# A two-layer image block: copies moved to one queue, and a new order of the second layer's steps

## The chip, the cores and the metric

The kernel runs on one core of a Trainium2 chip. The metric is the device time of one execution in microseconds (us). A core has five engines that run side by side, each in its own order of instructions: TensorE (PE, with its weight loads PEld), VectorE (DVE), ScalarE (ACT), GpSimd (POOL) and SyncE (SP), which here only issues transfers. Semaphores hold an instruction until what it needs is there.

## The reference, cut to what matters

32 images of 96 channels, 56 x 56. Two residual layers, each behind a group normalisation over three channels at a time:

```
# layer 0, on v = groupnorm(x): 4-bit weights and activations
h = act_q(bn(conv1x1(v, w1, 96 -> 576)))        # expansion
h = act_q(bn(depthwise3x3(h, w2)))
x = x + v + bn(conv1x1(h, w3, 576 -> 96))       # projection

# layer 1, on v = groupnorm(x): three parts of 32 channels; the gates come from means of v
a = conv3x3(v[:32],   conv0_w  * gate)          # spatial
F = frft2d(v[32:64], alpha)                     # fractional Fourier transform, alpha from an MLP
b = |frft2d(conv1x1([Re F, Im F], conv05_w * gate), -alpha)| / (56 * 56)
c = irfft2(conv1x1(rfft2(v[64:]), conv1_w * gate))
x = x + v + conv3x3([a, b, c], conv2_w)         # the finals
```

## The kernel before, in words

**Layer 0 of an image** works by phases: the 56 x 56 image is four images of 28 x 28 (even or odd row, even or odd column; `k` = 0 to 3). `norm` takes statistics of the input (L333). `split` writes the normalised phases into two tiles, `vh` and `vl`, whose sum is the value (L353 to L362); each has one buffer, so the next image's split can't start before this image's last expansion. `expand(b, k)` multiplies a phase with a block of 128 hidden channels (`b` = 0 to 4; block 4 has 64 real channels and 64 of zeros; L372), and `quant_act` takes the result out of PSUM: ScalarE scales and clips below into `qt` (L313), VectorE clips above into an FP8 tile (L315), here one of three `q1s` tiles. Then small copies (L385) rearrange it: 32 channels of one phase go to partitions 32k to 32k + 31 of a `qp` tile (three of these, used in turn by block), so that a depthwise step finds four phases of 32 channels on its 128 partitions. Copies with even group number are issued by SyncE, the others by GpSimd, 72 an image in all. `depthwise(b, j)` (L398) makes 32 of 576 channels, and again `quant_act` follows. `project` (L414) accumulates all 18 groups in PSUM, in two halves of the image, and VectorE adds the result to x (L426); `stats` takes layer 1's statistics of x (L430).

**Layer 1 of an image**: `means`, `gates` and `norm` (the head) give the statistics, the gates, and the normalised parts `xm`, `xf` and `xq`. `weights` makes the gated weights, `angles` the fractional matrices from alpha; its last result goes to two rows of `xf` by four small transfers (L603). `mix_t` and `hilbert` are the Fourier part, `spatial` the 3 x 3 part. The fractional part is `mix_f` (L653: a matmul for each of four pieces of each half image, a copy into a `zs` tile of two buffers, a transfer to `z` in DRAM), then transfers from `z` to `zh` (L663, one image row on each partition) and to `az` (L671), `rows_f` (L678), `columns_f` (L702) and `magnitude` (the roots, L720), which writes a third of `cat`. `final(j)` (L746, `j` = 0 to 6) is the last convolution of eight image rows, from `cat`, and VectorE adds it to x (L754). `store` writes x out (L757).

**Order.** Each step is an entry (cost, function), and `interleave(a, b)` merges two lists in proportion to summed cost. Layer 0 of image i runs beside layer 1 of image i - 1. For each image there are three stages: `conv` (18 depthwise steps and the expansions still missing, with the next image's `norm` and `split` put in) merged with layer 1's steps but the last four finals; `last` (project, stats) merged with two finals; then the head of layer 1 and the next image's first seven expansions (`LEAD`) with the last two finals and the store. The written order is not quite the executed one: the framework's scheduler places the instructions of each engine by its own estimate of times, and keeps what depends on what.

PSUM: `ps0` has two pairs of banks, which expansion, depthwise and projection share; `ps1` has four banks for the rest.

Of the kernel before, what the change touches and what calls it, by code (L numbers as in the profile page):

```python
# [63 lines left out]
LEAD = 7  # L64
L = 57
# [38 lines left out]
def block_kernel(ctx: ExitStack, tc: tile.TileContext, out: bass.AP, a: dict):  # L104
# [8 lines left out]
    p3 = ctx.enter_context(tc.tile_pool(name="p3", bufs=3))  # L113
    dp = ctx.enter_context(tc.tile_pool(name="dp", bufs=2, space=bass.MemoryType.DRAM))
# [28 lines left out]
    def prepare():  # L143
# [32 lines left out]
        w1 = cp.tile([C, NB * 128], F32R, tag="w1r", name="w1r")  # L176
        nc.vector.memset(w1f[:, HID:], 0.0)
        nc.vector.tensor_copy(w1, w1f)
# [74 lines left out]
    for k in range(3):  # L253
        t = cp.tile([128, PH, PW], FP8, tag=f"q1s{k}", name=f"q1s{k}")
        nc.gpsimd.memset(t, 0.0)
        q1s.append(t)
# [68 lines left out]
    def layer0(i):  # L325
# [42 lines left out]
        def expand(b, k):  # L368
            ps = pair(f"pe{i}_{b}_{k}")
            for n, v in enumerate((s["vh"], s["vl"])):  # L370
                for h in range(2):
                    nc.tensor.matmul(  # L372
                        ps[:, h, :HN],
                        w1[:, 128 * b : 128 * (b + 1)],
                        v[:, k, HN * h : HN * (h + 1)],
                        start=(n == 0),
                        stop=(n == 1),
                    )
            src = q1s[turn["q1s"] % 3]
# [53 lines left out]
        ex = [(0.75, lambda b=b, k=k: expand(b, k)) for b in range(NB) for k in range(4)]  # L433
# [16 lines left out]
    def layer1(i):  # L450
# [193 lines left out]
        def mix_f(j):  # L644

            if j == 0:
                s["z"] = dp.tile([128, 2, HH], F32, tag="z", name=f"z{i}")
            at = slice(HN * j, HN * (j + 1))
            for h in range(2):
                t = p2.tile([128, HN], F32, tag="zs", name=f"zs{i}_{j}_{h}")  # L650
                rows = slice(LOW * h, LOW * h + G + 2)
                ps = bank(ps1, f"pm{i}_{j}_{h}")
                nc.tensor.matmul(ps[:, :HN], g1[rows], s["xf"][rows, at], start=True, stop=True)  # L653
# [319 lines left out]
```

## Time and profile before

| | |
|---|---|
| median of 14 runs | 4777.9 us (4737.69 to 4801.65) |
| the profiled execution's own time | 4778.75 us |
| its span, first to last instruction | 4777.0 us |
| TensorE's mean granted clock | 0.942 |
| busy share: PE, DVE, ACT, POOL | 91%, 50%, 45%, 18% |
| finals (L746) on TensorE | 4032 instructions, 1650.9 us |
| depthwise (L398) on TensorE | 4608 instructions, 941.6 us |
| copies to qp (L385): SyncE, GpSimd | 1152 and 1152, of 26.2 KB each |
| longest chain of waits, share of the span | PE 62%, DMA 13%, DVE 10%, ACT 10% |

How to read it: an engine's line gives its busy time and what ended the idle time ahead of its instructions ("PE pi L678 <- DMA zh<-z" is TensorE waiting at line 678 for a transfer from z into zh). `pe`, `pd`, `pp`, `pm`, `pi`, `pz`, `ps` and `pc` are the PSUM results of expansion, depthwise, projection, fractional mix, rows, columns, spatial part and finals; `qte` and `qtd` are ScalarE's results of expansion and depthwise. The granted clock is the share of TensorE's full clock that its throttle let through; a matmul takes correspondingly longer. An instruction of TensorE shown as x18 for one final is nine taps with two passes each.

### The profile page before, as it was taken

What the parts mean: (1) busy time and instruction counts of PE and PEld (TensorE: products, weight loads), DVE (VectorE), ACT (ScalarE), POOL (GpSimd) and SP (SyncE); (2) the same over time, 40 slices, a digit from 0 to 9 for tenths busy, and PEclk for the clock granted to TensorE, in tenths of its full rate; (3) what the DMA queues carried; (4) which work ended last, traced back from release to release, by engine and by line L of the source; (5) the groups of instructions that cost most, each with busy time, mean ns of one, the idle gap of its engine ahead of it and who ended that gap; (6) DMA issues with size and microseconds to landing.
All of it is one profiled execution on the core that took longest, in us unless ns stands there. A gap on an engine that the chain in (4) does not pass through costs nothing.

```text
span 4777.0 us, 60944 instructions
## 1 busy us (share of the span) xinstructions
PE 4327.7 (91%) x21632; PEld 2505.7 (52%) x21632; DVE 2387.4 (50%) x5385; ACT 2168.1 (45%) x2824; POOL 859.5 (18%) x1361
## 2 busy tenths in 40 slices
PE   3899999999999999998999999999989989999987
PEld 2554555555555545555555555555555455555544
DVE  5545454545545544555455454555455444554532
ACT  3544445544445534455344454444454444553431
POOL 3221111221102211112211022211122111122100
PEclk9899999999999989999999999999999999999987
DMA  2221122221222211222212222112223112222112
GB/s 72 44 64 43 30 61 61 64 60 35 40 59 65 64 44 28 60 61 64 55 40 40 59 64 64 52 39 43 61 64 64 47 29 57 61 64 59 33 28 48
DMA packets 378818, 249.65 MB, mean 52 GB/s; under 512 B 283233, under 2 KB 371668, under 8 KB 372372
## 3 DMA queue, kind: packets, MB, share of 16 engines
q1 hardware_dynamic: 339072, 211.72, 20.2%
q0 software_dynamic: 36864, 31.04, 2.8%
q8 instruction: 174, 2.85, 0.3%
q10 hardware_dynamic: 2580, 2.99, 0.2%
q14 instruction: 128, 1.05, 0.1%
HBM read 92.90 MB, written 89.92 MB: 38 GB/s over the span
## 4 chain that ended last, share of the span: by engine, by line
PE 62%; DMA 13%; DVE 10%; ACT 10%; issue 3%; SPq 1%; POOL 1%; DVEq 0%; ACTq 0%; POOLq 0%
PE pc L746 33%; PE pd L398 11%; PE pp L414 5%; DMA z<-zs 5%; DMA zh<-z 4%; PE pe L372 4%; PE pi L678 3%; ACT cat L720 2%; ACT qte L313 2%; DMA xf<-vv 2%; ACT qtd L313 2%; DVE bn L333 2%; DVE x L426 2%; PE px L616 1%; DVE q1s L315 1%
## 5 line engine op out<-in xcount | busy, mean ns | idle before, releaser
L746 PE MATMUL pc<-cat,wc 96*96 96x448 f32 x4032 | 1650.9, 565 | 56.0 <-ACT cat L720 56.0
L385 POOL DMA_DIRECT2D qp<-q1s x1152 | 620.3, 542 | 3646.5 <-issue 1600.1
L746 PEld LDWEIGHTS pc<-cat,wc 96*96 96x96 f32 x4032 | 673.8, 170 | 911.7 <-issue 829.8
L313 ACT ACTIVATE qtd<-pd,o,s 128x784 int16<-128x784 f32 x576 | 577.0, 1002 | 941.0 <-PE pd L398 892.4
L398 PE MATMUL pd<-qp,dw 128*128 128x392 fp8e4 x4608 | 941.6, 349 | 41.5 <-ACT qtd L313 41.5
L313 ACT ACTIVATE qte<-pe,o,s 128x784 int16<-128x784 f32 x640 | 640.0, 1000 | 626.7 <-PE pe L372 608.7
L398 PEld LDWEIGHTS <-dw 128*128 128x128 fp8e4 x4608 | 446.7, 101 | 501.5 <-issue 257.5
L372 PE MATMUL pe<-vh,w1r 96*128 96x392 f32 x1280 | 432.8, 421 | 120.1 <-ACT qte L313 66.1
L315 DVE TENSOR_SCALAR q1s<-qte 128x784 fp8e4<-128x784 int16 x640 | 357.7, 559 | 175.0 <-ACT qte L313 125.2
L754 DVE SCALAR_TENSOR_TENSOR x<-pc,bc,x 96x448 f32<-96x448 f32 x224 | 152.3, 680 | 585.0 <-PE pc L746 582.5
L315 DVE TENSOR_SCALAR q<-qtd 128x784 bf16<-128x784 int16 x576 | 207.3, 360 | 398.8 <-ACT qtd L313 398.7
L372 PE MATMUL pe<-vl,w1r 96*128 96x392 f32 x1280 | 353.1, 358 | 0.0
L372 PEld LDWEIGHTS pe<-vh,w1r 96*128 96x128 f32 x1280 | 226.8, 200 | 238.3 <-issue 103.0
L414 PE MATMUL pp<-q,w3q 32*96 32x392 bf16 x4608 | 254.4, 327 | 2.2 <-DVE x L426 2.2
L372 PEld LDWEIGHTS pe<-vl,w1r 96*128 96x128 f32 x1280 | 247.4, 199 | 0.5
L653 PE MATMUL pm<-xf,g 34*128 34x392 f32 x512 | 187.8, 577 | 49.8 <-DMA xf<-vv 44.2
L426 DVE SCALAR_TENSOR_TENSOR x<-pp,s,x 96x392 f32<-96x392 f32 x256 | 142.3, 616 | 174.3 <-PE pp L414 174.3
L414 PEld LDWEIGHTS <-w3q 32*96 32x96 bf16 x4608 | 180.1, 117 | 85.8 <-issue 32.5
L678 PE MATMUL pi<-cs,zh 120*120 120x112 f32 x1024 | 157.7, 324 | 64.6 <-DMA zh<-z 62.1
L726 PE MATMUL ps<-xq,g 128*128 128x392 f32 x512 | 202.4, 538 | 0.0
L678 PEld LDWEIGHTS pi<-cs,zh 120*120 120x120 f32 x1024 | 152.6, 237 | 75.5 <-DVE q1s L315 29.5
L361 ACT CAST vh<-v 96x392 fp32r<-96x392 f32 x256 | 126.1, 515 | 131.8 <-DVE v L353 131.0
(150 smaller groups left out, 4052.3 us busy)
## 6 DMA issues: line engine op xcount, KB each, us to landing
z<-zs SPq DMA_DIRECT2D x256, 196.0 KB
x<-in_x_dram SPq DMA_DIRECT2D x32, 1176.0 KB
out_dram<-x SPq DMA_DIRECT2D x32, 1176.0 KB
qp<-q1s SPq DMA_DIRECT2D x1152, 26.2 KB
qp<-q1s POOLq DMA_DIRECT2D x1152, 26.2 KB, 1.9
zh<-z SPq DMA_DIRECT2D x64, 392.0 KB
az<-z SPq DMA_DIRECT2D x256, 98.0 KB
xf<-vv SPq DMA_DIRECT2D x128, 6.1 KB
```

The source lines that it names most:

```text
L313: nc.scalar.activation(t.rearrange("p (h n) -> p h n", h=2), ps[:, :, :HN], AF.Relu, bias=offset, scale=scale)
L315: nc.vector.tensor_scalar(dst, src, 15.0, None, ALU.min, saturate=False if dst.dtype == FP8 else None)
L372: nc.tensor.matmul(ps[:, h, :HN], w1[:, 128 * b : 128 * (b + 1)], v[:, k, HN * h : HN * (h + 1)], start=(n == 0), stop=(n == 1),)
L385: (nc.gpsimd if g % 2 else nc.sync).dma_start(out=qps[(NB * i + b) % 3][G * k : G * (k + 1), g, at : at + PH * PW], in_=src[g * G : (g + 1 ...
L398: nc.tensor.matmul(ps[:, h, :HN], dw[:, g, t, :], view(qps[(NB * i + b) % 3][:, j, :], at, [[PW, PH // 2], [1, PH]]), start=(t == 0), stop ...
L414: nc.tensor.matmul(s["pp"][k // 2][:C, k % 2, :HN], w3[rows, g, :], s["q2"][rows, g, HN * h : HN * (h + 1)], start=(g == 0), stop=(g == NG ...
L426: nc.vector.scalar_tensor_tensor(part, src, A3, part, ALU.mult, ALU.add)
L653: nc.tensor.matmul(ps[:, :HN], g1[rows], s["xf"][rows, at], start=True, stop=True)
L678: nc.tensor.matmul(ps[: LOW + W, 2 * W * k : 2 * W * (k + 1)], zh[:, c : c + 2, :].rearrange("p c w -> p (c w)")[:, : LOW + W], cs, start= ...
L726: nc.tensor.matmul(ps[:, :HN], s["g0"][:, 128 * k : 128 * (k + 1)], view(xq, PH // 2 * h * (W + 2) + k, [[W + 2, PH // 2], [2, PH]]), star ...
L746: nc.tensor.matmul(ps[:C, :CN], wc[:, C * t : C * (t + 1)], cat[:, CR * j + dy : CR * j + dy + CR, dx : dx + W], start=(t == 0), stop=(t = ...
L754: nc.vector.scalar_tensor_tensor(part, ps[:C, :CN], bc, part, ALU.add, ALU.add)
```

## The change

All copies to `qp` are issued by SyncE, and there are five `q1s` tiles (`NQ`) instead of three. The scratch space that the program reserves for descriptors of GpSimd's transfers is 1 KB instead of 16. Block 4 is packed: its weights lie between two blocks of zeros, so that four accumulated matmuls put phase k into the lower 64 rows of a PSUM pair and phase k + 1 into the upper 64; one `quant_act` takes both out, and there are 18 expansions an image instead of 20. (The per-channel vectors of block 4 are laid out twice to match, in a helper on the host's side that is left out below.)

In layer 1, `angles` comes ahead of `weights`; `mix_f` is eight steps, ordered by halves of the image, with its own pool of four `zs` buffers (shared with the columns' squares), and each half of `zh` is fetched as soon as its four pieces are written; both spatial steps come ahead of `hilbert`; the roots are taken in two halves, each behind two of the four column steps. Four finals (`HOLD`) are kept for the head instead of two, so one final instead of three lies in `conv`. The next image's statistics go in behind 16 entries of `conv` instead of 8, its split behind 22 instead of 26.

```diff
--- before.py
+++ after.py
@@ -62,6 +62,8 @@
 HH = HW // 2
 LOW = 64
 LEAD = 7
+NQ = 5
+HOLD = 4
 L = 57
 MAGIC = 1.5 * 2.0**23
 TWO_PI = 6.283185
@@ -111,6 +113,7 @@
     p1 = ctx.enter_context(tc.tile_pool(name="p1", bufs=1))
     p2 = ctx.enter_context(tc.tile_pool(name="p2", bufs=2))
     p3 = ctx.enter_context(tc.tile_pool(name="p3", bufs=3))
+    p4 = ctx.enter_context(tc.tile_pool(name="p4", bufs=4))
     dp = ctx.enter_context(tc.tile_pool(name="dp", bufs=2, space=bass.MemoryType.DRAM))
     ps0 = ctx.enter_context(tc.tile_pool(name="ps0", bufs=2, space=PSUM))
     ps1 = ctx.enter_context(tc.tile_pool(name="ps1", bufs=4, space=PSUM))
@@ -173,9 +176,11 @@
 
         w1f = load_tmp("w1")
         quantise(w1f, C, HID, "1")
-        w1 = cp.tile([C, NB * 128], F32R, tag="w1r", name="w1r")
-        nc.vector.memset(w1f[:, HID:], 0.0)
-        nc.vector.tensor_copy(w1, w1f)
+        w1 = cp.tile([C, NB * 128 + 64], F32R, tag="w1r", name="w1r")
+
+        nc.vector.memset(w1[:, HID - 64 :].bitcast(F32), 0.0)
+        nc.vector.tensor_copy(w1[:, : HID - 64], w1f[:, : HID - 64])
+        nc.vector.tensor_copy(w1[:, HID : HID + 64], w1f[:, HID - 64 : HID])
         w2 = load_tmp("w2")
         quantise(w2, 128, NG0 * 16, "2")
         mask = load_tmp("mask")
@@ -250,7 +255,7 @@
 
 
     q1s, qps = [], []
-    for k in range(3):
+    for k in range(NQ):
         t = cp.tile([128, PH, PW], FP8, tag=f"q1s{k}", name=f"q1s{k}")
         nc.gpsimd.memset(t, 0.0)
         q1s.append(t)
@@ -366,26 +371,31 @@
             nc.vector.tensor_scalar(xt, xt, s["one"], s["off"], ALU.mult, ALU.add)
 
         def expand(b, k):
+
             ps = pair(f"pe{i}_{b}_{k}")
-            for n, v in enumerate((s["vh"], s["vl"])):
+            m = blk(b)
+            n = 128 // m
+            for e in range(2 * n):
                 for h in range(2):
+                    at = 128 * b + m * (n - 1) * (1 - e // 2)
                     nc.tensor.matmul(
                         ps[:, h, :HN],
-                        w1[:, 128 * b : 128 * (b + 1)],
-                        v[:, k, HN * h : HN * (h + 1)],
-                        start=(n == 0),
-                        stop=(n == 1),
+                        w1[:, at : at + 128],
+                        s["vl" if e % 2 else "vh"][:, k + e // 2, HN * h : HN * (h + 1)],
+                        start=(e == 0),
+                        stop=(e == 2 * n - 1),
                     )
-            src = q1s[turn["q1s"] % 3]
+            src = q1s[turn["q1s"] % NQ]
             turn["q1s"] += 1
             quant_act(ps, A1[:, b : b + 1], B1[:, b : b + 1], src[:, :, :PH], f"e{i}_{b}_{k}")
 
-            n, at = blk(b) // G, PW * (k // 2) + k % 2
-            for g in range(n):
-                (nc.gpsimd if g % 2 else nc.sync).dma_start(
-                    out=qps[(NB * i + b) % 3][G * k : G * (k + 1), g, at : at + PH * PW],
-                    in_=src[g * G : (g + 1) * G].rearrange("c h w -> c (h w)"),
-                )
+            for u in range(128 // m):
+                at = PW * ((k + u) // 2) + (k + u) % 2
+                for g in range(m // G):
+                    nc.sync.dma_start(
+                        out=qps[(NB * i + b) % 3][G * (k + u) : G * (k + u + 1), g, at : at + PH * PW],
+                        in_=src[m * u + g * G : m * u + (g + 1) * G].rearrange("c h w -> c (h w)"),
+                    )
 
         def depthwise(b, j):
             g = 4 * b + j
@@ -430,7 +440,7 @@
                 nc.vector.bn_stats(stats2[i][:, j, :], xt[:, j * CN : (j + 1) * CN])
 
 
-        ex = [(0.75, lambda b=b, k=k: expand(b, k)) for b in range(NB) for k in range(4)]
+        ex = [(0.75, lambda b=b, k=k: expand(b, k)) for b in range(NB) for k in range(0, 4, 128 // blk(b))]
         de = [(1.45, lambda g=g: depthwise(g // 4, g % 4)) for g in range(NG0)]
         conv = []
         for g in range(NG0):
@@ -644,30 +654,29 @@
         def mix_f(j):
 
             if j == 0:
-                s["z"] = dp.tile([128, 2, HH], F32, tag="z", name=f"z{i}")
-            at = slice(HN * j, HN * (j + 1))
-            for h in range(2):
-                t = p2.tile([128, HN], F32, tag="zs", name=f"zs{i}_{j}_{h}")
-                rows = slice(LOW * h, LOW * h + G + 2)
-                ps = bank(ps1, f"pm{i}_{j}_{h}")
-                nc.tensor.matmul(ps[:, :HN], g1[rows], s["xf"][rows, at], start=True, stop=True)
-                if h:
-                    nc.vector.tensor_copy(t, ps[:, :HN])
-                else:
-                    nc.scalar.copy(t, ps[:, :HN])
-                nc.sync.dma_start(out=s["z"][:, h, at], in_=t)
-            if j < 3:
+                s["z"] = dp.tile([128, HW], F32, tag="z", name=f"z{i}")
+            h, k = divmod(j, 4)
+            rows = slice(LOW * h, LOW * h + G + 2)
+            ps = bank(ps1, f"pm{i}_{j}")
+            nc.tensor.matmul(ps[:, :HN], g1[rows], s["xf"][rows, HN * k : HN * (k + 1)], start=True, stop=True)
+            t = p4.tile([128, HN], F32, tag="zs", name=f"zs{i}_{j}")
+            if j % 2:
+                nc.vector.tensor_copy(t, ps[:, :HN])
+            else:
+                nc.scalar.copy(t, ps[:, :HN])
+            nc.sync.dma_start(out=s["z"][:, HN * j : HN * (j + 1)], in_=t)
+            if k < 3:
                 return
-            z = s["z"].rearrange("o u n -> o (u n)")
-            for k in range(2):
-                nc.sync.dma_start(
-                    out=zh[LOW * k : LOW * k + W, :, :W], in_=z[G * k : G * (k + 1)].rearrange("o (h w) -> h o w", w=W)
-                )
+            for t in range(2):
+                src = s["z"][G * t : G * (t + 1), HH * h : HH * (h + 1)].rearrange("o (h w) -> h o w", w=W)
+                nc.sync.dma_start(out=zh[LOW * t + PH * h : LOW * t + PH * (h + 1), :, :W], in_=src)
+            if h == 0:
+                return
             az = p1.tile([128, H // 4, 2, W], F32, tag="az", name=f"az{i}")
             s["az"] = az
             for r in range(4):
                 for t in range(2):
-                    src = z[2 * G + G * t : 3 * G + G * t].rearrange("o (q r w) -> r o q w", r=4, w=W)
+                    src = s["z"][2 * G + G * t : 3 * G + G * t].rearrange("o (q r w) -> r o q w", r=4, w=W)
                     nc.sync.dma_start(out=az[G * r : G * (r + 1), :, t, :], in_=src[r])
 
         def rows_f(g):
@@ -707,17 +716,18 @@
                     stop=True,
                 )
             m = 2 * W * n
-            sq = p2.tile([128, 8 * W], F32, tag="zs", name=f"sq{i}_{g}")
+            sq = p4.tile([128, 8 * W], F32, tag="zs", name=f"sq{i}_{g}")
             add = s["az"][:, 4 * g : 4 * g + n].rearrange("p q t w -> p (q t w)")
             nc.vector.tensor_tensor(sq[:, :m], ps[:, :m], add, ALU.add)
             nc.scalar.activation(sq[:, :m], sq[:, :m], AF.Square)
             z = sq[:, :m].rearrange("p (q r w) -> p q r w", r=2, w=W)
             nc.vector.tensor_tensor(s["Z"][:, 4 * g : 4 * g + n, :], z[:, :, 0, :], z[:, :, 1, :], ALU.add)
 
-        def magnitude():
+        def magnitude(h):
             dst = cat[G : 2 * G, 1 : 1 + H, 1 : 1 + W].rearrange("p (q r) w -> p q r w", r=4)
+            at = slice(8 * h, min(8 * h + 8, H // 4))
             for r in range(4):
-                nc.scalar.activation(dst[:, :, r, :], s["Z"][G * r : G * (r + 1)], AF.Sqrt)
+                nc.scalar.activation(dst[:, at, r, :], s["Z"][G * r : G * (r + 1), at], AF.Sqrt)
 
         def spatial(h):
 
@@ -760,10 +770,11 @@
             return [(c, lambda k=k: f(k)) for k in range(n)]
 
         first = [(0.5, means), (1.0, gates), (0.1, norm)]
-        steps = [(0.5, weights), (1.0, angles)] + each(1.1, mix_t, 4) + each(1.0, mix_f, 4)
-        sp = each(2.7, spatial, 2)
-        steps += sp[:1] + each(2.1, hilbert, 2) + each(1.3, rows_f, 4) + each(1.2, columns_f, 4)
-        steps += [(0.0, magnitude)] + sp[1:]
+        steps = [(1.0, angles), (0.5, weights)] + each(1.1, mix_t, 4) + each(0.6, mix_f, 8)
+        sp, co = each(2.7, spatial, 2), each(1.2, columns_f, 4)
+        steps += sp + each(2.1, hilbert, 2) + each(1.3, rows_f, 4)
+        for h in range(2):
+            steps += co[2 * h : 2 * h + 2] + [(0.1, lambda h=h: magnitude(h))]
         steps += each(6.7, final, NCH)
         return first, steps, [(0.0, store)]
 
@@ -777,15 +788,15 @@
         conv, nxt = now["conv"], None
         if i + 1 < B:
             nxt = layer0(i + 1)
-            conv[8:8] = nxt["norm"]
-            at = 2 * (4 * NB - LEAD) + 1
+            at = 2 * (4 * NB - 2 - LEAD)
             conv[at:at] = nxt["split"]
-
-
-        interleave(conv, one[:-4])
-        interleave(now["last"], one[-4:-2])
+            conv[at - 6 : at - 6] = nxt["norm"]
+
+
+        interleave(conv, one[: -HOLD - 2])
+        interleave(now["last"], one[-HOLD - 2 : -HOLD])
         head, two, done = layer1(i)
-        interleave(head + (nxt["first"] if nxt else []), one[-2:] + end)
+        interleave(head + (nxt["first"] if nxt else []), one[-HOLD:] + end)
         if i + 2 < B:
             load(i + 2)
         one, end, now = two, done, nxt
...
@@ -959,7 +969,7 @@
     import concourse.bacc as bacc
     from concourse.bass_utils import run_bass_kernel_spmd as run
 
-    nc = bacc.Bacc("TRN2", target_bir_lowering=False, num_devices=1)
+    nc = bacc.Bacc("TRN2", target_bir_lowering=False, num_devices=1, dynamic_dma_scratch_size=1024)
     arrays, args = {}, {}
     for name, v in _layout(inputs).items():
         v = np.ascontiguousarray(v)
```

More of the change, by code (lines that the diff above doesn't have):

```diff
@@ L887, in hidden @@
     def hidden(v):
-        p = np.zeros((NB * 128,) + v.shape[1:], f)
-        p[:HID] = v
+        p = np.concatenate([v, v[128 * (NB - 1) :]]).astype(f)
         return np.moveaxis(p.reshape((NB, 128) + v.shape[1:]), 0, 1)
```

## The prediction

> **What bounds the kernel now.** I read the engine table first, then TensorE's waits in the steady part (365.4 to 4575.1 us: 29 images, so 4209.7 / 29 = 145.2 us an image), then a table of short stretches of one image, then SyncE's queue. The engine table:
>
> ```profile
> PE 4327.7 (91%) x21632; PEld 2505.7 (52%) x21632; DVE 2387.4 (50%) x5385; ACT 2168.1 (45%) x2824; POOL 859.5 (18%) x1361
> ```
>
> TensorE sets the pace; nothing else passes half. So only TensorE's idle time and its clock can be won. Its waits in the steady part (line, awaited, us in total, times, longest):
>
> ```profile
> PE pi L678 <- DMA zh<-z: 56.1, 25, 3.5
> PE pe L372 <- ACT qte L313: 53.9, 18, 5.1
> PE pc L746 <- ACT cat L720: 49.6, 30, 1.7
> PE pm L653 <- DMA xf<-vv: 40.5, 28, 2.6
> PE pe L372 <- DVE x L426: 38.7, 29, 1.3
> PE pmb L295 <- DVE mvb L293: 26.1, 29, 0.9
> PE pd L398 <- ACT qtd L313: 22.4, 59, 0.5
> ```
>
> Each occurs about once an image: the transform's rows wait for zh, the first final for the roots, the fractional mix for xf, the end of layer 0 for its statistics. The second cost is the clock. In this table of stretches, after each stretch the columns are length, busy us of PE, PEld, DVE, ACT, POOL, then granted clock:
>
> ```profile
> 1216.00:1220.00 4.00, 0.60 (x5) 0.40 (x4) 1.45 (x3) 2.06 (x3) 0.50 (x1) 0.99 1.26 145
> 1220.00:1224.00 4.00, 4.00 (x24) 3.94 (x24) 0.77 (x2) 0.69 (x2) 0.00 (x0) 0.58 1.08 145
> 1236.00:1240.00 4.00, 2.34 (x11) 1.27 (x9) 0.24 (x1) 3.94 (x6) 0.00 (x0) 1.00 0.00 0
> 1240.00:1244.00 4.00, 4.00 (x8) 1.55 (x7) 3.64 (x8) 3.45 (x6) 0.68 (x1) 0.57 0.05 13
> 1296.00:1300.00 4.00, 4.00 (x10) 2.21 (x9) 1.80 (x7) 1.19 (x2) 3.98 (x8) 0.50 0.33 81
> ```
>
> A hole (first and third row) is followed by about 3.5 us at half clock: a stall costs its length and some 1.7 us more. I took such stretches of 28 images, aligned on their first final, and averaged idle time plus length x (1 - clock):
>
> - around zh: 1.73 + 1.46 = 3.2 us an image
> - around the first final: 1.65 + 0.90 = 2.5
> - around xf: 1.53 + 1.00 = 2.5
> - gates to angles: 1.30 + 1.33 = 2.6
> - statistics and head: 3.84 + 2.52 = 6.4
> - the rest: 0.5
>
> Together 17.7 of 145.2 us; the most that any reordering could bring is 31 x 17.7 = 550 us.
>
> [...] The trace has SyncE's issue at a median of 540 ns, GpSimd's at 496. [...]
>
> **The change part by part.**
>
> *Halved mix and copies of zh; root and transform order.* Now the rows wait for z<-zs and then 7.5 to 8.0 us of zh<-z (chain of waits). The 16 mixes, copies and z transfers stay the same in number and size. With the halves apart, the first pair of zh copies goes out after mix 3, the second after mix 7, so about 4 us of transfer follow the last mix. Both spatial steps and both Hilbert steps now lie between. The layer-1 steps ahead of the first final are 30.5 of 37.2 cost units spread over conv, before 29.5 of 49.6, so each has 1.4 times as much depthwise and expansion work beside it. Spatial 1 is moved from behind the rows to ahead of them: 3.0 us of TensorE more in the gap, against a wait of 1.9. Four zs buffers instead of two also remove VectorE's and ScalarE's waits for z (172.9 and 110.4 us in all). SyncE pays two more zh issues, 2 x 0.67. I take 85% of 3.2: **-2.7 us an image**; bounds 0 and -3.2.
>
> *Roots by halves.* Four roots of 868 ns and a table load of 1283 become eight of about half the size. From this trace's ScalarE copies (32x448 529 ns, 32x336 434) I estimate roots at 0.58 and 0.48 us: 4.2 us against 3.5, on an engine with 45% load. The first final waits only for the first half: 2.3 us of roots instead of 3.5, with two column steps (1.6 us) behind it on TensorE. 85% of 2.5: **-2.2**; bounds +0.5 (a second table load, were it needed, is 1.3 us) and -2.5.
>
> *Angles ahead of weights.* The weights' VectorE work (L534 to L558, 4.6 us in the tail) no longer delays the chain to xf, but px now waits for it instead; and the xf transfers share SyncE with a doubled stream of copies. Half of 2.5 at xf, and 0.3 of the 2.6 at the angles: **-1.5**; bounds +1 and -3.5.
>
> *Four finals held back, not two.* Finals 3 to 6, 6.9 us each, now run in the head, where expansions wait for ScalarE (53.9 / 29 = 1.9 us an image) while it writes xm and xq (3.4 us each pair). Two thirds of 1.9: **-1.2**. The hole at the statistics itself I leave: the instructions around it keep their order, and before, an available final was not put there. Bounds 0 and -6.
>
> *Statistics later, split earlier.* VectorE now waits 115.8 us in 31 pieces for x at L333, with copies out of PSUM queued behind it. Eight items later the load has landed. The split takes place when the last expansion has been issued, as vh and vl require. That gain is inside the xf and zh terms; 0 more, bounds +0.5 and -1.
>
> *Block 4 packed.* Eight matmuls for two phases as before, so TensorE keeps its work; 64 activations of 1000 ns and 64 VectorE copies of 559 ns go. Both are hidden by TensorE: **0**, bounds 0 and -1.
>
> *All copies on SyncE, five q1s buffers.* 1152 issues x 0.54 = 622 us move to SyncE, 19.4 us an image. With its 36 own copies (19.4), 8 z (2.6), 4 zh (2.7), 8 az (8.0 in a row), 4 xf (3.3) and two x transfers (0.7) SyncE issues 56 us in an image of 145: no bound on the mean. GpSimd gets its 620 us back, which nobody awaits. Ahead of each expansion's last copy lie 2.2 us of issue instead of 1.1. A copy behind zh and az waits about 12 us; before, the same happened to SyncE's half, and of the depthwise weights only one (0.6 us) waited for qp. Five buffers let VectorE write on meanwhile, where with three it waited 44.8 us. The 1 KB scratch space has no user left. With two finals gone from conv, ScalarE has there 29 activations of 1.0 us, 4.1 of splits, about 19.5 of layer 1 and 3 between instructions, 56 us; TensorE has 18 depthwise steps of 1.38, 11 expansions of 0.93, 27 of layer 1 and a final of 6.9, 69 us. So I add **+0.5** for new waits for ScalarE and copies; bounds -1 and +9.
>
> Sum: -2.7 - 2.2 - 1.5 - 1.2 + 0.5 = -7.1 an image, x 31 = -220. The last image's layer 1 has no cover (waits of 6.6 us for angles, 4.6 for zh, 3.4 for roots); I take 8 of these 14.6: -8. Together **-228** against the profiled execution's own 4778.75 us: 4551. That execution is 0.85 us above the median of 14, so I say **4550**.
>
> **The rivals.**
>
> *A. As worked out,* 4550, its own range 4470 to 4630 (5 to 10 us an image). For it: three separate holes, each with its cover visible.
>
> *B. The holes move.* The order that is executed is not the order written, since a scheduler places each engine's instructions by its own estimate; and transforms with fewer finals beside them may now wait for ScalarE (startup, with only depthwise and expansion, shows 0.38 us idle in every 2.64). A third of the gain, 2.5 us an image: 4778 - 78 = 4700. Against it: conv's ratio of ScalarE to TensorE, 56 to 69, is no worse than in the stretch that now runs almost without such waits.
>
> *C. SyncE's queue blocks the depthwise: slower.* Where conv alternates a depthwise and an expansion every 2.64 us, a block's last expansion is four such steps (10.5 us) ahead of its use; activation, copy, issue and landing (1.0 + 0.6 + 2.2 + 1.9) leave 4.8. Queued behind a zh wait, four zh and eight az (some 12 us), it would be late by 7 us, and the clock adds 1.7. Nearly 9 us lost outweigh the 7.6 gained: with both xf and zh waiting behind copies as well (their 2.7 lost) the balance is +4 us an image, 4778 + 124 = 4900; at half that, 4840. It decides as soon as that lateness passes 7 us. Against it: the layer-1 steps between make four items 14 to 16 us.
>
> *D. The head's hole closes too,* since four finals are at hand: 4 of 6.4 us more, 31 x 4 = 124: 4425.
>
> **How the numbers follow.** A 0.58, B 0.20, D 0.10, C 0.12. A and D are faster; B is faster by over 0.3% (14 us, about what a measurement of this kernel can tell from no change) in 0.17 and the same in 0.03; C's mildest part joins B: slower 0.11, same 0.04, faster 0.85. The range leaves out most of C, half of D and little of B: **4430 to 4720**.
>
> **What would show it.** Right: waits of PE for zh and for cat under 15 us each, PE's clock at 0.96 or more, PE busy at 94% or above, POOL without copies, ScalarE's qte at 576. Wrong: PE's loads at L398 waiting for qp (C), pd or pe waiting for qtd or qte for over 100 us (B). The pmb wait should stand at about 26 us; if it goes, D. A clock that stays at 0.94 in spite of fewer holes would refute the link between the two.

## The result, and the profile after

The changed kernel takes **4893.1 us** (median of 10 runs, 4877.5 to 4907.7) against 4775.1 of the kernel before on the same chips: ratio **1.0243**, 95% interval 1.0223 to 1.0264. It is 2.4% slower; the forecast was 4550 and faster. The profiled span is 4883.3 us (before 4777.0), the mean clock 0.915 (0.942).

The engine table of the changed kernel, and its waits of TensorE in the steady part (365 to 4700 us; columns as before):

```profile
PE 4468.1 (91%) x21632; PEld 2624.6 (54%) x21632; DVE 2369.7 (49%) x5322; ACT 2148.9 (44%) x2888; POOL 182.9 (4%) x211
```
```profile
PE pc L756 <- ACT cat L730: 99.9, 29, 3.7
PE pm L661 <- DMA qp<-q1s: 38.9, 11, 4.2
PE pm L661 <- DMA xf<-vv: 35.3, 11, 3.9
PE pe L381 <- DVE x L436: 34.7, 29, 1.2
PE pp L424 <- DVE x L436: 32.0, 29, 1.1
PE pm L661 <- issue: 22.5, 7, 3.4
PE pd L408 <- ACT qtd L318: 10.4, 29, 0.4
PE pmb L300 <- DVE mvb L298: 8.8, 29, 0.9
```

TensorE issues the same 21632 matmuls but is busy 140 us longer. The wait for zh (56.1 us) is gone, and so is that for qte. The roots' wait has doubled (49.6 to 99.9), and the wait ahead of the mixes (L661) went from 40.5 to 97 us over three releasers: DMA on two names, and "issue". (The mixes read no qp; such a name is only that of the transfer that landed last.)

A table of stretches around one image's mixes shows the second cost (columns: stretch, length, busy us of PE, PEld, DVE, ACT, POOL, clock, DMA share, GB/s):

```profile
1216.00:1220.00 4.00, 2.40 (x14) 1.49 (x12) 1.14 (x3) 3.15 (x5) 0.00 (x0) 1.00 0.97 239
1220.00:1222.00 2.00, 0.00 (x0) 0.00 (x0) 0.29 (x1) 0.00 (x0) 0.00 (x0) 1.00 0.37 56
1222.00:1226.00 4.00, 3.97 (x8) 1.90 (x8) 4.00 (x9) 0.97 (x2) 0.00 (x0) 0.65 0.25 77
1226.00:1230.00 4.00, 4.00 (x13) 2.33 (x12) 1.43 (x4) 0.77 (x1) 0.00 (x0) 0.50 0.52 175
1234.00:1238.00 4.00, 4.00 (x13) 2.86 (x12) 0.37 (x2) 2.01 (x2) 0.00 (x0) 0.64 0.98 265
```

After a hole of 3.6 us the clock is halved for over 6 us, and again at 1234, where PE has no hole at all.

To place the loss I cut the trace of every kernel at the first matmul of six steps, image by image, and averaged over 26 to 29 images the idle time and the clock loss, length x (1 - clock), in us an image (other choices of images move an entry by about 0.1):

| from / to | before: idle + clock | changed: idle + clock | difference |
|---|---|---|---|
| angles / mixes | 1.44 + 0.02 | 3.42 + 0.00 | +2.0 |
| mixes / rows | 2.19 + 1.42 | 0.36 + 5.37 | +2.1 |
| rows / first final | 1.70 + 1.32 | 3.45 + 0.15 | +0.6 |
| first final / projection | 0.00 + 0.94 | 0.00 + 2.47 | +1.5 |
| projection / statistics | 2.38 + 0.00 | 2.74 + 0.85 | +1.2 |
| statistics / angles | 3.28 + 3.84 | 0.00 + 4.02 | -3.1 |

Sum +4.3 an image; the rest of an image, PE busy at full clock, is equal (126.8 and 126.6 us). So the whole loss is idle time and clock loss, and of the two it is the clock loss: over the execution idle fell from 449 to 415 us while clock loss rose from 275 to 415.

### The profile page after: what moved, and what is told of

Same layout as the page of the kernel before. It is cut to its first block, busy times and chain, and to the rows that moved or that the text cites. A ratio compares the mean times of both kernels' runs of the same rounds, so it can differ in the third digit from the quotient of the medians.

```text
span 4883.3 us, 59704 instructions
## 1 busy us (share of the span) xinstructions
PE 4468.1 (91%) x21632; PEld 2624.6 (54%) x21632; DVE 2369.7 (49%) x5322; ACT 2148.9 (44%) x2888; POOL 182.9 (4%) x211
## 4 chain that ended last, share of the span: by engine, by line
PE 83%; DVE 7%; ACT 4%; DMA 3%; issue 2%; SPq 1%; ACTq 0%; DVEq 0%; POOL 0%
PE pc L756 35%; PE pd L408 15%; PE pe L381 8%; PE pp L424 6%; PE pm L661 5%; PE ps L736 4%; DVE x L436 2%; PE pi L687 2%; PE px L626 2%; DMA xf<-vv 2%; ACT cat L730 1%; DVE bn L440 1%; PE pr L644 1%; PE pr L641 1%; ACT L730 1%
## 5 line engine op out<-in xcount | busy, mean ns | idle before, releaser
L756 PE MATMUL pc<-cat,wc 96*96 96x448 f32 x4032 | 1726.1, 588 | 109.9 <-ACT cat L730 109.9
L756 PEld LDWEIGHTS pc<-cat,wc 96*96 96x96 f32 x4032 | 706.0, 178 | 1016.7 <-issue 890.4
L318 ACT ACTIVATE qte<-pe,o,s 128x784 int16<-128x784 f32 x576 | 574.5, 1003 | 809.2 <-PE pe L381 791.1
L320 DVE TENSOR_SCALAR q1s<-qte 128x784 fp8e4<-128x784 int16 x576 | 321.9, 563 | 256.5 <-ACT qte L318 219.9
L661 PE MATMUL pm<-xf,g 34*128 34x392 f32 x512 | 247.1, 641 | 102.8 <-DMA xf<-vv 41.4
L424 PE MATMUL pp<-q,w3q 32*96 32x392 bf16 x4608 | 291.7, 327 | 35.3 <-DVE x L436 35.3
L661 PEld LDWEIGHTS pm<-xf,g 34*128 34x128 f32 x512 | 112.6, 231 | 198.9 <-issue 150.9
L338 DVE BATCH_NORM_STATS2 bn<-x 96x6 f32<-96x448 f32 x224 | 121.1, 608 | 113.8 <-DMA x<-in_x_dram 113.8
L748 DVE TENSOR_SCALAR cat<-ps,b 32x392 f32<-32x392 f32 x128 | 79.9, 624 | 141.3 <-ACT cat L750 141.3
L736 PEld LDWEIGHTS ps<-xq,g 128*128 128x128 f32 x512 | 103.1, 202 | 80.7 <-issue 79.6
```

Source lines behind the costliest of these rows:

```text
L318: nc.scalar.activation(t.rearrange("p (h n) -> p h n", h=2), ps[:, :, :HN], AF.Relu, bias=offset, scale=scale)
L320: nc.vector.tensor_scalar(dst, src, 15.0, None, ALU.min, saturate=False if dst.dtype == FP8 else None)
L338: nc.vector.bn_stats(stats[:, j, :], xt[:, j * CN : (j + 1) * CN])
L424: nc.tensor.matmul(s["pp"][k // 2][:C, k % 2, :HN], w3[rows, g, :], s["q2"][rows, g, HN * h : HN * (h + 1)], start=(g == 0), stop=(g == NG ...
L661: nc.tensor.matmul(ps[:, :HN], g1[rows], s["xf"][rows, HN * k : HN * (k + 1)], start=True, stop=True)
L736: nc.tensor.matmul(ps[:, :HN], s["g0"][:, 128 * k : 128 * (k + 1)], view(xq, PH // 2 * h * (W + 2) + k, [[W + 2, PH // 2], [2, PH]]), star ...
```

## The experiments

The theories, which the expectations call by these letters or by their words: **S**, SyncE's queue delays the copies (the forecast's rival C); **R**, the mixes contract over only 34 rows, and so few rows let the clock fall; **H**, the transfers of xf are held up by the load of x; and that the earlier split (**P**) or the held finals open the new holes.

**The copies alone.** The kernel before, with this part only:

```diff
-    for k in range(3):
+    for k in range(NQ):          # NQ = 5
-                (nc.gpsimd if g % 2 else nc.sync).dma_start(
+                nc.sync.dma_start(
-    nc = bacc.Bacc("TRN2", target_bir_lowering=False, num_devices=1)
+    nc = bacc.Bacc("TRN2", target_bir_lowering=False, num_devices=1, dynamic_dma_scratch_size=1024)
```

> The kernel before with the first part of the change alone: all copies to qp issued by SyncE, five q1s tiles, 1 KB of scratch space; block 4 and layer 1 as before. Theory S (SyncE's queue is what got slower): slower than before by 50 us or more, with TensorE's weight loads or matmuls of the depthwise waiting for qp. Theories R and H (the new order is at fault): within 15 us of before, 4760 to 4790, and a granted clock of 0.94.

4714.9 us, ratio 0.9882 (0.9853 to 0.9911): **1.2% faster**, better than either case expected. S falls: one queue costs nothing. In its waits, steady part, the wait for zh is small and the first line is new; the third is SyncE's own wait ahead of issuing xf's transfers:

```profile
PE pm L654 <- DVE bn L334: 104.2, 28, 4.8
PE pi L679 <- DMA zh<-z: 13.9, 12, 2.0
```
```profile
SPq L604 <- DMA x<-in_x_dram: 85.0, 28, 3.7
```

VectorE, in order, waits at L334 for x's load, and so does SyncE with xf's transfers: here too the wait of the mixes leads back to the load of x. Cut by steps as above, this kernel already has the longer hole ahead of the mixes (3.66) and the larger clock loss behind it (5.38), with the mixes in the old order, and it has most of the gain at the head: from statistics to angles 1.33 idle + 1.70 clock are left of 3.28 + 3.84. The slowdown is in what is left of the change (block 4, layer 1, and the places of statistics and split): 4893 - 4715 = 178 us. In the same cut this lies between the rows and the next angles.

**Four held finals, or two?** The changed kernel with

```diff
-HOLD = 4
+HOLD = 2
```

> The changed kernel with two finals held for the head instead of four (HOLD = 2). In the executed order of TensorE the mixes then stand as 2, 2, 2, 2 steps between depthwise steps and expansions instead of 4 and 4, and three pairs of depthwise and expansion follow the last final before the angles, where the changed kernel has none. If holding four finals is what made the groups of low activity and brought xf's transfers together with the load: clock 0.935 or more, the wait at L661 below 60 us, and 4893 - 31 x 5 = 4700 to 4780. If only the wait for xf changes: 4800 to 4840. If neither depends on the held finals: 4893 within 20.

4955.2 us, ratio 1.0347 (1.0311 to 1.0384), 62 us slower still, outside all three cases expected. The loss from statistics to angles is 5.15 us an image against 4.02 with four, and the clock loss behind the mixes 8.77 against 5.37. So holding four pays on balance, though not without a price, as the last experiments show.

**Rows of the mixes.** The changed kernel with weights padded by zeros to 128 rows (one tile for each half) and one xf tile of 128 rows, cleared once:

```diff
-            nc.tensor.matmul(ps[:, :HN], g1[rows], s["xf"][rows, HN * k : HN * (k + 1)], start=True, stop=True)
+            nc.tensor.matmul(ps[:, :HN], g1s[h], xf[:, HN * k : HN * (k + 1)], start=True, stop=True)
```

> The changed kernel with the fractional mixes (L661) contracting over all 128 partitions instead of 34: the added rows of xf and of the weights are zeros, xf is a constant tile, and nothing else is moved; the result is the same sum and a matmul of 392 columns streams as long. Theory R (once the clock has fallen at the hole ahead of the mixes, [...] groups of eight of them keep the clock at half or lower it again): clock up from 0.915 to 0.93 or more, 60 to 130 us faster than the changed kernel, 4760 to 4830, with the hole ahead of the mixes as long as it was (about 100 us in all at L661). Theory H (only holes count, the rows don't): 4893 within 15 us and a clock of 0.915.

4779.7 us, ratio 1.0008 (0.9996 to 1.0021): 113 us back with nearly four times the multiplications. The hole ahead of the mixes is still there (3.70 us), but the clock loss behind it falls from 5.37 to 1.40. R holds. (Four us an image, times 29, are about the 113.) Where the clock is up, a matmul of the mixes takes as long with either: a median of 489 ns with 34 rows and 492 with 128, in 16 and 32 instructions of two kernels below.

**The clock by itself.** Matmul streams without gaps, nothing else of the computation kept, one execution:

```python
stream(34 rows fp32); stream(128); stream(34); stream(128); stream(64)
stream(128); stream(96 rows, 96 columns); stream(128); stream(32 rows bf16)
stream(128); four groups of 32 rows bf16 in turn; stream(128)
```

> A stream of matmuls alone, without waits, of 392 columns each: 60 with 34 rows, 40 with 128, again 60 and 40, 60 with 64 rows, 40 with 128, 60 with 96 rows and 96 columns of weights, 40 with 128, 200 of bf16 with 32 rows, 40 with 128, 400 of bf16 with 32 rows in four row groups in turn, 40 with 128. All of the reference's computation is left out. Theory R: the clock stays or goes to about 0.5 in the stretches of 34 and of 32 rows and is 1.0 in those of 128. Theory H: after the first few us the clock is 1.0 in all of them.

Groups of its instructions (tile, weights, shapes, count | busy, mean ns | idle), then stretches of its trace (columns as above, without ACT): 128, 34, 34, 64 and 96 rows in fp32, 32 rows in bf16, four groups in turn.

```profile
L121 PE MATMUL ps<-xt 128*128 128x392 f32 x480 | 165.8, 508 | 0.0
L121 PE MATMUL ps<-xt 34*128 34x392 f32 x240 | 153.9, 840 | 6.0 <-DMA xt<-in_x_dram 6.0
L121 PE MATMUL ps<-xt 64*128 64x392 f32 x120 | 39.8, 490 | 0.0
```
```profile
100.00:110.00 10.00, 10.00 (x32) 5.76 (x31) 0.00 (x0) 0.00 (x0) 1.00 0.00 0
120.00:130.00 10.00, 10.00 (x17) 5.15 (x16) 0.00 (x0) 0.00 (x0) 0.50 0.00 0
180.00:190.00 10.00, 10.00 (x16) 4.75 (x15) 0.00 (x0) 0.00 (x0) 0.50 0.00 0
240.00:250.00 10.00, 10.00 (x32) 5.70 (x31) 0.00 (x0) 0.00 (x0) 1.00 0.00 0
300.00:310.00 10.00, 10.00 (x31) 4.89 (x30) 0.00 (x0) 0.00 (x0) 1.00 0.00 0
370.00:380.00 10.00, 10.00 (x32) 6.08 (x31) 0.00 (x0) 0.00 (x0) 0.50 0.00 0
450.00:460.00 10.00, 10.00 (x108) 6.53 (x108) 0.00 (x0) 0.00 (x0) 1.00 0.01 2
```

PE is busy for all of every stretch, and with 34 or 32 rows it still runs at half clock: with 34 rows 16 or 17 instructions in 10 us (each fp32 matmul is two: the program's 240 with 128 rows show as 480) where 64, 96 and 128 rows have 31 or 32. The 32 of the bf16 stretch are at half clock as well; before the clock fell they came faster (42 from 350 to 360 us, at a mean clock of 0.67). The clock falls 3.7 us after the second 34-row stretch begins (114.1 to 117.8) and as long after the bf16 stretch does. It returns 5.8 us after the first 34-row stretch ends, 3.7 after the second (189.2 to 192.9) and 3.3 after the bf16 one. Four groups of 32 rows in turn keep it up.

**xf's transfers from ScalarE.** The changed kernel with

```diff
-                    nc.sync.dma_start(
+                    nc.scalar.dma_start(
                         out=s["xf"][at : at + 1].rearrange("p (h w) -> p h w", w=W),
```

> The changed kernel with the four small transfers to xf issued by ScalarE instead of SyncE, where three of them stand behind the load of a whole image. Theory H (the mixes start late because xf's data queue behind that load and the copies; the hole costs its length and the clock): TensorE's wait at L661 falls from 103 us to under 45, some 2 us an image of hole and 2 to 4 of clock, so 4893 - 31 x 5 = about 4740 to 4790. Theory R alone: the hole closes as well, but the clock still drops within the mixes, so only about half of that, 4800 to 4840. If the transfers are late for another reason [...], no change.

4815.8 us, ratio 1.0097 (1.0069 to 1.0124), 77 us back, but not where it was meant: the hole ahead of the mixes is 3.67 us, as before the edit; what fell was idle time ahead of the first final (3.45 to 1.51) and clock. Queueing on SyncE is not what delays xf. Why the roots gained shows in the trace: with ScalarE's order changed, the scheduler put the next image's split elsewhere. Of 28 images, 5 still have five casts of that split (L366) ahead of the first roots, and a hole of 3.4 us there; the other 23 have none, and holes of 1.0 to 1.1. The first final of one image of either kind:

```profile
836.29 7.76 PE L756 MATMUL pc<-cat,wc 96*96 96x448 f32 x20 [1.13 <-ACT cat L730]
1420.20 10.09 PE L756 MATMUL pc<-cat,wc 96*96 96x448 f32 x19 [3.43 <-ACT cat L730]
```

So most of these 77 us belong to the split's place, which the next experiment changes alone.

**The split later.** The changed kernel, the split behind 26 entries of `conv` again:

```diff
-            conv[at:at] = nxt["split"]
+            conv[at + 4 : at + 4] = nxt["split"]
```

> The changed kernel with the next image's split four entries of conv later, as before the change (behind 26 entries, statistics still behind 16). In the executed order of ScalarE the five casts to vh that stood ahead of the first roots then stand behind the second ones; the mixes keep their groups of eight. Theory P (the split takes ScalarE and VectorE in front of the roots and lengthens the hole ahead of the first final from 1.7 to 3.4 us): TensorE's wait at L756 for the roots falls from 110 us to 55 or less, and with the clock 31 x 2.5 to 3.5 = 80 to 110 us are gained: 4785 to 4815. Theories R and H alone: 4893 within 15 us.

4689.1 us, ratio 0.9792 (0.9762 to 0.9822): **204 us back**, the largest single part and twice what was expected. With this one list position restored, the change is 2.1% faster than the kernel before, not 2.4% slower. ScalarE's order in the changed kernel shows the cause (start, us, instruction), and the waits of the two lines after the edit what became of it:

```profile
1263.19 0.93 ACT L366 CAST vh<-v 96x392 fp32r<-96x392 f32 x2
...
1266.11 0.52 ACT L366 CAST vh<-v 96x392 fp32r<-96x392 f32 x1 [0.29 <-DVE v L358]
1266.80 0.94 ACT L366 CAST vh<-v 96x392 fp32r<-96x392 f32 x2 [0.18 <-DVE v L358]
1267.76 1.28 ACT L730 ACT_TABLE_LOAD   x1
1269.06 2.36 ACT L730 ACTIVATE cat<-Z 32x448 f32<-32x448 f32 x4
```
```profile
PE pc L756 <- ACT cat L730: 29.3, 30, 1.2
PE pp L424 <- DVE x L436: 6.4, 30, 1.1
```

Three of the five casts of the next image's split stand between the last square that the first roots need and those roots, and TensorE waits 3.4 us. VectorE has steps of the same split there too (L358, L367); which of the two engines counts more, no run separates. With the split behind the roots the hole is 0.98 us instead of 3.45, and the clock loss between first final and projection (2.47) is gone.

**Two repairs together, and three.** 128 rows with xf from ScalarE:

> The changed kernel with both edits that were tried singly: mixes over 128 partitions (alone 113 us faster) and xf's transfers issued by ScalarE (alone 77 us faster). If the two are one effect (the clock at the mixes, which falls at the hole): 4760 to 4790, no more than the rows alone. If they add up (the hole's own length, some 2 us an image, is on top): 4700 to 4740.

4637.9 us, ratio 0.9673 (0.9642 to 0.9703), 255 us below the changed kernel where the parts make 190, and below both cases expected. In its trace no cast of the split stands ahead of the first roots in any of 28 images, so the edit at xf has moved the split here in all images. With the later split as well:

> All three repairs at once in the changed kernel: mixes over 128 rows, the transfers of xf issued by ScalarE, the split four entries later. With the first two alone it took 4637.9 us (0.967 of before), and there the loss ahead of the roots and up to the projection was already down to 1.13 us an image of idle time and nothing of clock (changed kernel 3.45, and 2.47 of clock). If the late split repairs that same place, little is left for it: 30 to 100 us, 4540 to 4610. If it acts by itself, as it did in the changed kernel (204 us), 4430 to 4460. If the later split now collides with the mixes, it is not faster than 4637.

4598.4 us, ratio 0.9639 (0.9596 to 0.9681): 40 us more, at the upper end of the first case. The later split and xf from ScalarE repair the same place, as the casts show, so they do not add.

**128 rows in the old order.** The kernel with the copies alone, and 128 rows; then the same with the next image's statistics behind 16 entries as well:

> The kernel before with all copies on SyncE and five q1s (layer 1 in the order of before, statistics and split where they were), and the mixes over 128 rows. Row theory: between the mixes and the columns its 5.38 us an image of clock loss fall to about 1.5, as in the changed kernel with 128 rows, and the time from 4714.9 to 4580 to 4620. If the loss there comes from the hole of 3.66 us ahead of the mixes and not from their rows, no change: 4700 to 4725. The comparison with the changed kernel with 128 rows (4779.7) then tells what the new order of layer 1 is worth with the row effect gone: slower than this one means that the order itself costs.

> A candidate: the kernel before with all copies on SyncE and five q1s tiles (alone 4715), the next image's statistics behind 16 entries of conv, and mixes over 128 partitions. In the copies alone TensorE waits at the mixes 108 us for VectorE's statistics, which wait for the load of x; later statistics should remove 31 x 3 of hole and clock, the rows another 20 to 60 of clock. Theories R and H together: 4560 to 4650. If the statistics only move the hole elsewhere: 4680 to 4720.

4782.2 us (1.0016, 0.9998 to 1.0033) and 4778.3 (0.9988, 0.9972 to 1.0003). Both missed: 128 rows in the old order made it 67 us **slower** than the copies alone. The clock loss from mixes to rows did fall (5.38 to 2.30), but idle time there rose from 0.57 to 2.35, ahead of the mixes from 3.66 to 4.48, and the wait for zh from 13.9 to 55.5. A faster mix seems to end there in a longer wait for the transfers of a whole zh. That it is the halved zh of the new order which lets the repair count is argued, not shown: no run changes it alone. Why it ends 67 us worse than even stays open.

**The load of x.** What is common to the kernels with four held finals so far: the mixes start 0.2 to 0.6 us (median of 26 images) after x has landed, whoever issues xf. SyncE's issues, kernel before and changed kernel, one image each (start, us of issue):

```profile
1323.67 0.35 SPq L757 DMA_DIRECT2D out_dram<-x  x1
...
1330.47 0.34 SPq L130 DMA_DIRECT2D x<-in_x_dram  x1
...
1333.95 3.29 SPq L603 DMA_DIRECT2D xf<-vv  x4
```
```profile
1207.05 0.35 SPq L767 DMA_DIRECT2D out_dram<-x  x1
...
1212.84 0.83 SPq L613 DMA_DIRECT2D xf<-vv  x1
1213.79 0.44 SPq L133 DMA_DIRECT2D x<-in_x_dram  x1
1214.29 2.41 SPq L613 DMA_DIRECT2D xf<-vv  x3
```

Relative to the first matmul of the angles, the store moved from -5.1 to +0.8 us and the load, which waits for the store's buffer, from +1.2 to +7.4 (medians of 25 images). That is what two more held finals do: the image is finished later (with two held in the new order the figures are -4.9 and +1.4). The load of 1176 KB now runs over xf's 6 KB pieces, and the trace's record of DMA packets shows it: the last of xf's 112 packets ends 3.9 us after the last of its issues (median of 26 images), with ScalarE issuing them 5.3. A first attempt gave x a fourth buffer and wrote the load earlier (with two zs buffers to make room):

> The changed kernel with the load of the image after next issued at the head of an image's list, behind nothing, instead of right after the store in the middle of xf's four transfers; x has four buffers for it, and the zs pool two instead of four to make room. If the store and the load share the DMA engines with xf's transfers and hold them up, the idle time between the angles and the mixes falls from 3.42 us an image to 1.5 to 2, the wait of VectorE for x's load (113.8 us) goes, and the time falls by 40 to 80 us, the half clock at the 34-row mixes staying: 4810 to 4850. If the hole is the length of the chain angles, copies, weights, transfers itself, it stays at 3.0 to 3.6 and the time within 20 us of 4893.

4824.3 us, ratio 1.0109 (1.0073 to 1.0145), hole 3.28: it does not test H, since the load stood at the same place of the queue, now for an image later. The 69 us come with the smaller zs pool and the order around it. Most of them are clock loss behind the mixes (5.37 to 3.59), whose second group of eight instructions now stands as six and two; the two edits were not taken apart. The same with all three repairs:

> The three repairs and the early load of x together. If the hole ahead of the mixes is the load's, 40 to 80 us below the kernel with the three repairs alone, and idle between angles and mixes under 2 us an image. If not, within 20 us of it. It is the candidate for the fastest version: 4480 to 4600.

4563.2 us, ratio 0.956 (0.9524 to 0.9597), 35 us below the three repairs alone and so between the two cases; the load stands beside xf's transfers here as well. Then the load was moved for good. Buffers as in the last two runs; the edit is shown against the changed kernel:

```diff
+        if i + 2 < B:
+            conv.insert(24, (0.0, lambda k=i + 2: load(k)))
...
-        if i + 2 < B:
-            load(i + 2)
```

> The kernel with the early load (4824.3 us, in which the load still stood between the first and the second of xf's four transfers in SyncE's queue, and the mixes started 0.4 us after x had landed), with the load given out at the end of the depthwise list instead: in the queue it now stands behind all four xf transfers and the first three stores of mixed rows. If the mixes wait because xf's small transfers end only when the load of 1.18 MB beside them ends, the hole between angles and mixes falls from 3.28 us of idle time an image to 1 to 2, the start of the mixes after the last of xf's issues falls from 5.1 us to about 2, and the time to 4730 to 4780. If the hole is the chain's own length, or the store of the finished image is what fills the engines, hole and time stay (4800 to 4840). Third: the load now lies over the stores of mixed rows and the transfers of zh, and the wait moves to the columns' inputs: the hole falls, the time doesn't.

4722.4 us, ratio 0.9894 (0.9868 to 0.9920), 102 us below the kernel whose load stands between, a little better than expected. SyncE's queue, and the waits for the mixes in the steady part:

```profile
1184.90 3.25 SPq L613 DMA_DIRECT2D xf<-vv  x4
...
1195.34 1.00 SPq L667 DMA_DIRECT2D z<-zs  x2
1196.43 0.39 SPq L133 DMA_DIRECT2D x<-in_x_dram  x1
```
```profile
PE pm L661 <- DMA xf<-vv: 5.6, 18, 1.2
PE pm L661 <- DVE PQ L632: 1.0, 2, 0.5
PE pm L661 <- issue: 1.0, 5, 0.2
```

xf's last packet now ends 0.8 us after the last issue, the mixes start 0.6 us after it instead of 5.1 (the first of them need only the first and third transfer), and the hole falls from 3.28 to 0.29 us. **H holds**, in this form: xf's transfers end late while the load runs beside them, on whichever queue; the run with xf from ScalarE agrees (3.67 us). The DMA share was 0.97 from 1216 to 1220 in the changed kernel, under the load; here it is 0.12 and 0.14 over xf's transfers (1184 to 1188 and 1188 to 1192) and 0.99 under the load (1196 to 1200). Which DMA engine carried which packet no trace shows, so how the load delays them stays open. With the hole gone the clock loss after it falls from 3.59 to 1.52, though the mixes still have 34 rows; they also stand in smaller groups, so this is not the hole's alone. Over the runs cut this way the pattern is clear: 34 rows behind a hole of 3.3 us or more lost 3.6 to 8.8 us of clock an image, in two groups or spread over four; 34 rows behind 1.4 us or less lost 1.4 to 1.5, and 128 rows behind 3.7 to 4.6 lost 1.4 to 2.5. Here, where the mixes are short, it takes the hole and the thin matmuls together to hold the clock down for long. Last, this with 128 rows and the later split, all issued by SyncE:

> Mixes over 128 rows, the split four entries later, and the load behind xf's transfers, all issued by SyncE. If the load is what holds xf up, this is the fastest version: the kernel with the first two, xf on ScalarE and the load ahead of it took 4563.2 us; 3.35 us of idle time an image ahead of the mixes falling to 1 to 2 gives 4480 to 4530. If not, 4550 to 4580, and above it if the load now delays the columns.

**4413.3 us**, ratio **0.9252** (0.9232 to 0.9272), the fastest version, better than the range expected. Its engine table and its waits for mixes and roots:

```profile
PE 4134.4 (94%) x21632; PEld 2475.7 (56%) x21632; DVE 2367.7 (54%) x5324; ACT 2130.4 (48%) x2888; POOL 190.3 (4%) x212
```
```profile
PE pm L665 <- DMA xf<-vv: 34.1, 28, 2.2
PE pc L760 <- ACT cat L734: 29.1, 30, 1.0
```

An image has 4.8 us of idle time and 3.0 of clock loss left, against 9.97 and 12.87. The parts, each against its own control, are 69 (buffers), 102 (load), 113 (rows) and 204 (split): 4893 - 488 = 4405, and 4413 was measured. The 8 us between them flatter the sum, since the times come from different chips: by the ratios, each against the kernel before beside it, the parts make 10.35% and the whole 9.91%. Nor did the parts add in the runs with xf from ScalarE. What the 69 us consist of stays without a shown cause.

## Why the prediction was wrong, point by point

- *Bound.* Right: TensorE sets the pace, and the loss is idle time and clock alone.
- *Halved mix and zh, -2.7.* The wait went as said (56.1 us to nothing; idle 2.19 to 0.36), but most of that came with the copies alone (0.57). The 4 us of transfer behind the last mix were an estimate, half of 7.5 to 8.0; from its first issue to its last packet a pair of halved zh transfers took 3.1 us (median of 58 pairs), a pair of whole ones in the kernel before 6.3 (of 29). The term is wrong by the clock: +3.95 us an image there. The sum priced every hole at its length and a fixed tail of about 1.7 us of lost clock. The tail depends on what runs in it, here the 34-row mixes, and on the hole, now 2.0 us longer. That they stand closer is not the reason: the copies alone lost as much (5.38) with the mixes spread.
- *Roots by halves, -2.2.* Idle rose by 1.75 instead. Halving worked (2.36 us of roots after the table load, predicted 2.3); the step that failed is what stands ahead of it on ScalarE. With the split later the hole is 0.98 against 1.70 before.
- *Statistics later, split earlier, "0 more", bounds +0.5 and -1.* **The step that failed**: the split's place, priced at nothing, costs 204 us, 6.6 an image, more than the whole slowdown of 118. I asked what the split needs, and not whom its casts delay: on ScalarE they stand ahead of the roots. The later statistics brought little: VectorE still waits for x at L338, 113.8 us against 115.8, and in the old order they made 4 us (4782.2 to 4778.3; in ratios 1.0016 to 0.9988).
- *Angles ahead of weights, -1.5.* The hole grew by 2.0, as it did with the copies alone. The chain is in fact quick (0.6 us from the last issue, once the load no longer stands beside it), so what ended the wait was the load of x, which the prediction did not have here. What the step itself is worth, no run shows.
- *Four finals held, -1.2.* The head gained more, -3.1, but the copies alone, with two finals held, gained 4.1 there: the wait for qte that this term was to cover went with them. Between two and four in the new order it is 1.1 us an image (5.15 to 4.02), about the forecast. But I moved the finals without the store and the load that follow them, 6 us later and onto xf's transfers. "Bounds 0 and -6" excluded a loss without a reason.
- *Copies on SyncE, +0.5.* Alone -60 us, -1.9 an image. Rival C is refuted: in the changed kernel TensorE's weight loads waited for qp 3.4 us in all and its depthwise matmuls 6.0. That 4893 lies beside C's 4900 is chance. Block 4 packed: 0 is not separated, the changed waits do not show it.
- *The rivals.* B, the holes move, named the right kind of outcome, with too small a price: moved holes were taken to keep a third of the gain, not to cost more than the old ones. Its tell-tale, pd and pe waiting for ScalarE over 100 us, was not what happened. D came half true (the wait at pmb fell from 26.1 to 8.8) and was outweighed.
- *The link between holes and clock.* The sentence that a clock staying at 0.94 would refute it was to the point: less idle time, yet 0.915. In the stream of 34 rows it fell after 3.7 us with no idle time at all, and with 64 and 96 rows it stayed at 1.00: being busy is not enough, the rows count too.

## What to carry to other kernels

When an edit moves a step, follow each thing that it issues or releases: here the load behind a store behind two finals, and five casts on an engine that nobody called a bottleneck, cost more than the wait that was removed. An edit of one engine's list can also move work elsewhere, as xf's transfers moved the split: look where it went before naming a cause. A repair that loses in one order (128 rows in the old one, 67 us) can be worth 2% in another, so try it again after each step. And take the clock as a cost of its own: thin matmuls near a hole are dearer than their rows suggest (34 rows lost 5.37 us of clock an image behind a hole of 3.42, 128 rows 1.40 behind 3.70).

## What the runs showed of the hardware

- Matmuls over 34 or 32 rows back to back let the clock fall to 0.50 after 3.7 us, with no idle time at all; 64, 96 or 128 rows, or four groups of 32 rows in turn, hold it at 1.00. In a stream, 128 rows then take half as long as 34 (32 instructions against 16 in 10 us). Rows of zeros count too: with them the clock loss behind the mixes fell from 5.37 to 1.40 us an image.
- The last packet of four transfers of 6.1 KB, issued around a load of 1176 KB, ended 3.9 us after their last issue instead of 0.8, and 5.3 when ScalarE issued them beside SyncE's load.
